# Cosine attention: queries and keys turned by 32x32 blocks and DMA instead of on TensorE, and output products held until after a projection's keys

## The chip, the cores and the metric

The kernel runs on one core of a Trainium2 chip (trn2). A core has TensorE (PE: matmuls; PEld: its weight loads), VectorE (DVE), ScalarE (ACT), GpSimd (POOL) and SyncE (SP, whose queue issues all the DMAs here). Each has its own list of instructions and works through it in order; waits between engines go by semaphores. The metric is the device time of one execution in microseconds (us). All data is float32.

## The reference

Four layers run one after the other on x of 8 batches x 256 rows x 512 features: a conditioned attention with MLP, a cosine attention with MLP, a sparse attention, and a layer of small experts. The change lies in the second layer's attention, 16 heads of 32 features:

```python
qkv = (xin @ Wqkv.T + qkv_bias).reshape(Bs, Lx, 3, H, D)
q, k, v = (qkv[0], qkv[1], qkv[2])
sm = jnp.exp(jnp.minimum(scale_mul_log, jnp.log(jnp.float32(100.0))))
qn = q / jnp.maximum(jnp.linalg.norm(q, axis=-1, keepdims=True), 1e-12) * sm
kn = k / jnp.maximum(jnp.linalg.norm(k, axis=-1, keepdims=True), 1e-12)
scores = jnp.einsum('bhqd,bhkd->bhqk', qn, kn) + attn_bias
p = jax.nn.softmax(scores, axis=-1)
o = jnp.einsum('bhqk,bhkd->bhqd', p, v)
return o @ Wproj.T + bproj
```

The layer adds this, times a factor gamma1 per batch and feature, to x.

## The kernel before

One Python program lays out the whole work. A tile framework allots buffers, sets the semaphores, and may reorder independent instructions on an engine by its own estimate of times; `keep_in_program_order` pins an instruction at its place on its engine. A buffer kind has a fixed number of copies (line 42): PSUM, where TensorE writes, has four banks "A" for scores and four banks "C" for everything else; hT, qT, kT and v have two copies each.

`attend` (line 655) runs an attention layer. Its main loop (line 838) goes over batch b and head group g: for the cosine layer 8 batches, and 4 groups of 4 heads. An iteration computes the scores of its group (`scored`, line 685: for each of two query tiles a product of 128 queries with 256 keys for each head, L697; the four heads fill the four A banks), then the softmax (line 706). There DVE adds the bias and takes the row minimum of the negated scores, reading an A bank (L743), and ACT exponentiates and sums (L747). To be weighted with the values the weights must be turned, keys to the partitions. For two of the four heads of a group (in all batches but the last) that goes over DRAM: DVE turns 32x32 blocks (L752), four DMAs write the tile to a DRAM buffer with the blocks rearranged (`put`, line 545, L549), and one fetches it back (L756); this is called a flip below. The other heads are turned on TensorE (L783). One group later the weighting follows (L808), and the division by the sums (L830).

Between these steps `some(us)` (line 208) takes work from a queue of generators, each of which yields its estimated time; `todo` us are planned per batch and spread over its steps. At the first group of a batch `rest` empties the queue. For the cosine layer the queue holds the projection of the next batch (`project1`, line 1458) and the output products of the last one (`finish`, line 1546), put at the queue's front when the last group has been weighted (line 909).

`project1` takes the input hT of its batch (normalised, turned by blocks over DRAM in `prepare` and `fetch`, and scaled in place in `modulate`, L490 and L491). For both tiles t of 128 rows it makes the products for queries and keys (L631), adds the query bias on DVE (L1495), squares on ACT (L1496, L1498), sums per head on DVE (L1501), raises to the power -0.5 on POOL (L1504), and scales on POOL (L1508). Then it makes the values (copied on ACT, L1516), and turns queries and keys on TensorE: `turned` (line 1476), four turns of 128x128 into one C bank (L1479), copied out alternately by DVE (L480) and ACT (L483) to qT and kT with features on the partitions. `finish` adds a bias to the output product on DVE (L1454) and gates and adds to x on POOL (L1455, L1456). The first batch is projected at the end of the first layer's MLP (`layer1_begin`, line 1582), with 22.1 us planned.

Of the kernel before, what the change touches and what calls it, by code (L numbers as in the profile page):

```python
# [27 lines left out]
F32 = mybir.dt.float32  # L28
# [60 lines left out]
ROUND = 1.5 * 2.0**23  # L89
PI_BELOW = 3.1415925  # L90


# [87 lines left out]
class Program:  # L180
# [50 lines left out]
    def setup(self):  # L231
# [39 lines left out]
        self.turns = [self.tc.dram_tile([P, KC * S], F32, name=f"turn{i}") for i in range(3)]  # L271
        self.n_turn = 0
        self.flips = [self.tc.dram_tile([P, 8 * P], F32, name=f"flip{i}") for i in range(4)]
        self.n_flip = 0
# [270 lines left out]
    def put(self, kept, tile):  # L545

        to = kept.rearrange("(c i) (a x) -> a i c x", c=4, a=4)
        for a in range(4):
            self.nc.sync.dma_start(  # L549
                to[a], tile[32 * a : 32 * a + 32, :].rearrange("p (c x) -> p c x", c=4)  # L550
            )

    def fetch(self, calls):

        for (name, b), entry in self.ready.items():
            hT, _, kept, _, _ = entry
# [98 lines left out]
    def attend(self, name, n_groups, hd, project, value, finish, work, key_tiles=(2, 2), biased=None,  # L655
               extra=None, then=None, spare=None, inverse=None, after=None, rooms=None, contexts=None):

# [27 lines left out]
        def scored(b, g):  # L685
# [3 lines left out]
            for j0 in range(0, 4, rows):  # L689
                for q in range(TB):  # L690
                    for j in range(j0, j0 + rows):
                        lhsT, rhs = lhs_rhs[j]
                        keys = rhs(wide[q])
                        if j < self.in_blocks(name, b):

                            keys = keys.rearrange("p (k c i) -> p c k i", c=4, i=32)
                        mm = nc.tensor.matmul(  # L697
# [122 lines left out]
        def divided(b, o, by):  # L820
            for c in range(nch):
                chunks = ctx.setdefault(b, [])
                if b == late:
                    out = spare()[len(chunks)]
                elif contexts is not None:
                    out = contexts[:, b % 2 * 4 + len(chunks), :]
                else:
                    out = self.t([P, S], "ctxT")
# [9 lines left out]
        for i in range(B * n_groups + 1):  # L838
# [59 lines left out]
            else:  # L898
# [368 lines left out]
    def project0(self, b, got):  # L1267
# [32 lines left out]
        def scores(g, j):  # L1300
# [3 lines left out]
                lambda q: qT[rows, c, q * P : (q + 1) * P],  # L1304
                lambda n: kT[rows, 0:n],
            )
# [49 lines left out]
    def layer0_mlp(self):  # L1356
# [54 lines left out]
        def finish(hh, b, ys):  # L1411
# [8 lines left out]
            lambda b: self.h("mlp0", b), finish,  # L1420
            (self.layer1_begin(), 22.1),
        )
# [35 lines left out]
    def project1(self, b, got):  # L1458
# [16 lines left out]

        def turned(t, y, yT, at):
            m = self.bank("C")
            for c in range(KC):
                nc.tensor.transpose(  # L1479
                    m[:, c * P : (c + 1) * P], y[:, c * P : (c + 1) * P], self.ident  # L1480
                )
# [4 lines left out]
        ready = []  # L1486
        for t in range(TB):
            ss = self.t([P, 32], "ss", 2)
            both = []
            for i in range(2):  # L1490
# [18 lines left out]
                both.append(y)  # L1509
            ready.append(both)  # L1510
        qT = self.t([P, KC, S], "qT")
        kT = self.t([P, KC, S], "kT")
        v = self.t([P, TB, D], "v")
        for t in range(TB):
            vp = yield from part(t, 2)
            nc.scalar.copy(v[:, t, :], vp)  # L1516
            if t == 0:
                turned(0, ready[0][0], qT, 0)
                yield 0.43
                turned(0, ready[0][1], kT, 1)  # L1520
                yield 0.43
        yield None
        turned(1, ready[1][0], qT, 0)
        yield 0.43
        turned(1, ready[1][1], kT, 1)
        yield 0.43

        def scores(g, j):
            rows = slice(32 * j, 32 * j + 32)
            return (  # L1530
                lambda q: qT[rows, g, q * P : (q + 1) * P],
                lambda n: kT[rows, g, 0:n],
            )
# [3 lines left out]
    def layer1_attention(self):  # L1537
# [128 lines left out]
    def project2(self, b, got):  # L1666
# [29 lines left out]
        def scores(g, j):  # L1696
            rows = slice(32 * j, 32 * j + 32)
            return (
                lambda q: qT[rows, g, q * P : (q + 1) * P],
                lambda n: kT[rows, 0:n],  # L1700
            )
# [4 lines left out]
    def layer2(self):  # L1706
# [10 lines left out]
            inverse=[spare[:, i, :] for i in range(4, 8)],  # L1717
            rooms=self.rooms, contexts=contexts,
        )
# [280 lines left out]
```

## Time and profile before

| | |
|---|---|
| median of three runs | 2081.69 us (2081.62 to 2082.62) |
| the profiled execution's own time | 2078.34 us |
| its span | 2076.6 us |
| cosine attention, groups of scores | from 907.2 us to some 1245 us |
| one batch in its middle | 43.66 us |
| TensorE's granted clock in the stage | 1.00 of full speed |
| busy in such a batch | PE 43.53, DVE 29.79, ACT 26.36, POOL 23.3 us |
| L1479, turns on TensorE | 128, records of 273 ns |
| L752, L534, block turns on DVE, 128x1024 | 1245 ns each |
| L1504, power on POOL, 128x16 | 32, 2931 ns each |
| L1508, scaling on POOL, 128x512 | 32, 1050 ns each |
| DMA in the stage | 54 to 55% of 16 engines, 141 GB/s |

A line Lnnn is a line of the kernel's text. An entry "PE C L631" is work of TensorE that writes to banks C, issued by line 631. A float32 product leaves two matmul records, a turn one. Records of matmuls overlap, so what one costs is read from the distance of their starts; and a busy PE may be waiting between records. In the chain of waits each piece is what the end of the work hung on at that time.

### The profile page before, as it was taken

How to read it: one execution, taken by the hardware profiler on the slowest of the kernel's cores; microseconds unless marked ns; L12 is line 12 of the kernel's file. 1: busy time of each engine (PE TensorE's matmuls, PEld its weight loads, DVE VectorE, ACT ScalarE, POOL GpSimd, SP SyncE). 2: the span in 40 equal slices, each digit the busy share in tenths (PEclk: the TensorE clock that was granted, in tenths of full speed). 3: DMA queues.
4: the chain of work that ended last, by engine and by line, in shares of the span. 5: the costliest groups of instructions: out<-in, count | busy, mean ns of one | idle time of the engine just before them, and what ended most of it. 6: DMA issues, size and time to landing. Idle time of an engine off the chain costs nothing.

```text
span 2076.6 us, 36333 instructions
## 1 busy us (share of the span) xinstructions
PE 2006.0 (97%) x12818; PEld 1480.9 (71%) x12818; DVE 1365.2 (66%) x4429; ACT 748.1 (36%) x2332; POOL 334.0 (16%) x372
## 2 busy tenths in 40 slices
PE   7999999999999999999999999999999989989999
PEld 4555579999999999954544447999999854445454
DVE  6867766656675555656676766776765678776544
ACT  4333421111111111136565653222222256565644
POOL 1111200000000000054544531000000021101411
PEclk9999999999999999999999999999999989999999
DMA  8543361112130010334555543233211245653411
GB/s 306 166 119 90 102 215 48 65 42 64 61 110 26 17 31 16 96 99 129 131 143 141 141 123 115 89 101 116 87 60 48 67 113 137 158 145 97 126 40 42
DMA packets 223685, 208.91 MB, mean 101 GB/s; under 512 B 83536, under 2 KB 184976, under 8 KB 223120
## 3 DMA queue, kind: packets, MB, share of 16 engines
q1 hardware_dynamic: 223504, 206.59, 34.3%
q8 instruction: 102, 1.67, 0.3%
q14 instruction: 79, 0.65, 0.1%
HBM read 135.46 MB, written 71.07 MB: 99 GB/s over the span
## 4 chain that ended last, share of the span: by engine, by line
PE 78%; DVE 7%; ACT 7%; DMA 4%; issue 2%; POOL 2%; SPq 1%; DVEq 0%; ACTq 0%; POOLq 0%
PE C L1024 29%; PE A L1073 18%; PE C L631 17%; PE A L697 3%; ACT p L747 3%; PE C L808 3%; ACT wbig L747 2%; PE C L783 2%; PE C L1887 2%; PE A L1789 1%; DMA turn<-hT 1%; PE C L1822 1%; DVE st L449 1%; DMA wbig<-in_wgT 1%; DVE n L650 1%
## 5 line engine op out<-in xcount | busy, mean ns | idle before, releaser
L1024 PE MATMUL C<-hT,wbig 128*128 128x128 f32 x3072 | 416.4, 275 | 0.0
L1024 PEld LDWEIGHTS C<-hT,wbig 128*128 128x128 f32 x3072 | 388.8, 192 | 9.0 <-issue 2.4
L631 PE MATMUL C<-wqkv,hT 128*128 128x512 f32 (+1 forms) x768 | 316.6, 553 | 0.9 <-ACT v L1516 0.4
L1073 PE MATMUL A<-wbig,p 128*128 128x256 f32 x1024 | 242.2, 379 | 0.0
L631 PEld LDWEIGHTS C<-wqkv,hT 128*128 128x128 f32 x768 | 134.0, 195 | 122.8 <-issue 108.5
L1073 PEld LDWEIGHTS A<-wbig,p 128*128 128x128 f32 x1024 | 189.7, 190 | 23.1
L1054 DVE TENSOR_TENSOR p<-p,C 128x256 f32<-128x256 f32 x192 | 79.3, 421 | 162.5 <-PE C L1024 160.8
L1044 ACT COPY p<-C 128x128 f32<-128x128 f32 x192 | 51.3, 267 | 370.3 <-PE C L1024 361.8
L1024 PE MATMUL C<-qk,wbig 128*128 128x128 f32 x1152 | 160.0, 275 | 0.0
L1024 PE MATMUL C<-ctxT,wbig 128*128 128x128 f32 x1152 | 160.0, 275 | 0.0
L457 POOL TENSOR_SCALAR r<-mv 128x2 f32<-128x2 f32 (+1 forms) x28 | 7.1, 254 | 929.0 <-DVE mv L450 929.0
L747 ACT ACTIVATE p<-p,low 128x256 f32<-128x256 f32 x256 | 127.3, 501 | 69.9 <-DVE low L743 48.4
L1024 PEld LDWEIGHTS C<-qk,wbig 128*128 128x128 f32 x1152 | 144.1, 192 | 0.0
L1024 PEld LDWEIGHTS C<-ctxT,wbig 128*128 128x128 f32 x1152 | 144.1, 192 | 0.0
L747 ACT ACTIVATE wbig<-wbig,low 128x128 f32<-128x128 f32 (+1 forms) x256 | 113.7, 448 | 78.9 <-DVE low L743 75.9
L1398 ACT ACTIVATE p<-C 128x128 f32<-128x128 f32 x64 | 17.8, 278 | 294.9 <-DVE p L1054 294.9
L1045 DVE TENSOR_TENSOR p<-p,C 128x128 f32<-128x128 f32 x192 | 55.0, 286 | 97.5 <-ACT p L1044 96.4
L631 PE MATMUL C<-wo,ctxT 128*128 128x512 f32 x224 | 103.1, 600 | 1.2 <-DVE ctxT L830 1.2
L1504 POOL TENSOR_TENSOR ss<-ss,neg_half 128x16 f32<-128x16 f32 x32 | 93.8, 2931 | 2.7
L747 ACT ACTIVATE p<-A,low 128x256 f32<-128x256 f32 x128 | 59.3, 486 | 87.0 <-DVE low L727 75.9
L697 PE MATMUL A<-kT,qT 32*128 32x256 f32 (+2 forms) x896 | 85.9, 399 | 1.4 <-ACT p L747 0.6
L697 PEld LDWEIGHTS A<-kT,qT 32*128 32x128 f32 (+1 forms) x896 | 52.4, 191 | 41.9 <-issue 29.0
(268 smaller groups left out, 3507.6 us busy)
## 6 DMA issues: line engine op xcount, KB each, us to landing
flip<-p SPq DMA_DIRECT2D x160, 128.0 KB
p<-flip SPq DMA_DIRECT2D x40, 512.0 KB
turn<-hT SPq DMA_DIRECT2D x120, 128.0 KB
flip<-wbig SPq DMA_DIRECT2D x112, 96.0 KB
wbig<-flip SPq DMA_DIRECT2D x28, 384.0 KB
hT<-turn SPq DMA_DIRECT2D x16, 512.0 KB
kept<-hT SPq DMA_DIRECT2D x16, 512.0 KB
hT<-kept SPq DMA_DIRECT2D x16, 512.0 KB
```

Source lines behind the costliest of these rows:

```text
L631: self.nc.tensor.matmul(out, lhsT(k), rhs(k), start=(k == 0), stop=(k == n - 1))
L697: mm = nc.tensor.matmul(s[j][:, at[q] : at[q] + wide[q]], lhsT(q), keys, start=True, stop=True,)
L747: nc.scalar.activation(out, src, AF.Exp, bias=low[:, q : q + 1], scale=sign, accum_out=tot[:, j, q : q + 1],)
L783: nc.tensor.transpose(m[:, n * P : (n + 1) * P], p[:, at[q] + k * P : at[q] + (k + 1) * P], self.ident,)
L808: mm = nc.tensor.matmul(o[i * hd : (i + 1) * hd, c * S + q0 * P : (c + 1) * S], value(got[b][1], g, j, k), weights(j, mine), start=(k == 0 ...
L1024: nc.tensor.matmul(m[:, c : c + P], w[:, k * P : (k + 1) * P], b[:, k], start=(first and k == 0), stop=(k == steps - 1), skip_group_check= ...
L1044: nc.scalar.copy(g[:, 0, :], m[:, 0:P])
L1045: nc.vector.tensor_tensor(g[:, 0, :], g[:, 0, :], m[:, P : 2 * P], ALU.add)
L1054: nc.vector.tensor_tensor(g[:, 1:3, :], g[:, 0, :].unsqueeze(1).to_broadcast([P, 2, P]), m[:, 2 * P : 4 * P].rearrange("p (i t) -> p i t", ...
L1073: nc.tensor.matmul(acc[at][:, half * S : (half + 1) * S], left, right, start=(p == 0 and half == 0), stop=(p == 3), skip_group_check=True,)
L1504: nc.gpsimd.tensor_tensor(r, r, self.neg_half[:, 0:16], ALU.pow)
L1887: nc.tensor.matmul(m[:, half * S : half * S + S], left[:, r, i, :], right[:, i, :], start=(first and i == 0), stop=(i == 1), skip_group_ch ...
```

## The change

Queries and keys of a projection are no longer turned on TensorE. POOL's scaling writes each row tile's queries and keys into one tile of 128x1024, ordered in 32-wide blocks: the tile of qT for the first 128 rows, that of kT for the others. DVE turns the 32x32 blocks of each such tile, and four DMAs write it to a DRAM buffer (`pairs`). The tile of the first rows is turned right after queries and keys; that of the second when 3.3 us (by the planner's count) of what follows have been given out. At 5.0 us four DMAs fetch: the queries of each row tile into a tile "qk", the keys of both into kT. At 9.0 us POOL copies the queries from there to qT. What is left at the projection's end is done then. The DVE turns and the POOL copies are pinned in program order. Keys stay in block order in kT, and the scores read them through a view in pieces of 32.

What follows queries and keys in a projection is now first the output products of the batch before, which `attend` holds back in `between` instead of putting them at the queue's front (for batches up to 5), and then the values. The contexts that wait for their output product lie in nine spare places in the second MLP's weight tiles, no longer in "ctxT". The projection is planned with 20.5 us instead of 22.1.

```diff
+def keys_of(keys, blocks):
+    return keys.rearrange("p (k c i) -> p c k i", c=4, i=32) if blocks else keys
...
+    def outputs_between(self):
+        while self.between:
+            yield from self.between.pop(0)
+
+    def turned_blocks(self, tile, kept):
+        self.tc.keep_in_program_order(self.nc.vector.transpose(tile, tile))
+        self.put(kept, tile)
...
-                        keys = rhs(wide[q])
-                        if j < self.in_blocks(name, b):
-                            keys = keys.rearrange("p (k c i) -> p c k i", c=4, i=32)
+                        keys = rhs(wide[q], j < self.in_blocks(name, b))
...
-                            self.queue.insert(0, outcome(b))
+                            if split and b + 2 < B:
+                                self.between.append(outcome(b))
+                            else:
+                                self.queue.insert(0, outcome(b))
...
-        def turned(t, y, yT, at):
-            m = self.bank("C")
-            for c in range(KC):
-                nc.tensor.transpose(
-                    m[:, c * P : (c + 1) * P], y[:, c * P : (c + 1) * P], self.ident
-                )
-            self.copy(
-                t + at, yT[:, :, t * P : (t + 1) * P], m.rearrange("p (c q) -> p c q", c=KC)
-            )
...
+        stages = [self.t([P, KC * S], tag) for tag in ("qT", "kT")]
+        keeps = [self.pairs[(self.n_pair + t) % 4] for t in range(TB)]
+        self.n_pair += TB
         for t in range(TB):
+            put = stages[t].rearrange("p (c w k i) -> p w k c i", c=4, w=2, k=KC)
...
-                by = r.unsqueeze(2).to_broadcast([P, 16, 32])
-                nc.gpsimd.tensor_tensor(heads(y), heads(y), by, ALU.mult)
+                by = r.rearrange("p (k c) -> p k c", c=4).unsqueeze(3)
+                nc.gpsimd.tensor_tensor(
+                    put[:, i], y.rearrange("p (k c i) -> p k c i", k=KC, c=4),
+                    by.to_broadcast([P, KC, 4, 32]), ALU.mult,
+                )
+        qT, kT = stages[0].rearrange("p (k t) -> p k t", k=KC), stages[1]
         v = self.t([P, TB, D], "v")
+        self.turned_blocks(stages[0], keeps[0])
+
+        def others():
+            yield from self.outputs_between()
+            for t in range(TB):
+                vp = yield from part(t, 2)
+                nc.scalar.copy(v[:, t, :], vp)
+
+        came = []
+        def fetched():
+            for t in range(TB):
+                kept = keeps[t].rearrange("p (a w x) -> p w a x", a=4, w=2)
+                came.append(self.bank("qk"))
+                nc.sync.dma_start(came[t].rearrange("p (a x) -> p a x", a=4), kept[:, 0])
+                nc.sync.dma_start(
+                    kT.rearrange("p (t a x) -> p t a x", t=TB, a=4)[:, t], kept[:, 1]
+                )
+        def placed():
+            for t in range(TB):
+                copy = nc.gpsimd.tensor_copy(
+                    qT[:, :, t * P : (t + 1) * P].rearrange("p k (a j) -> p k a j", a=4),
+                    came[t].rearrange("p (a k j) -> p k a j", a=4, k=KC),
+                )
+                self.tc.keep_in_program_order(copy)
+
+        way = [(3.3, lambda: self.turned_blocks(stages[1], keeps[1])), (5.0, fetched), (9.0, placed)]
+        done = 0.0
+        for us in others():
+            yield us
+            done += us or 0.0
+            while way and done >= way[0][0]:
+                way.pop(0)[1]()
+        for _, do in way:
+            do()
...
-            "attention1", 4, 32, self.project1, value, finish, (22.1, 6.8),
+            "attention1", 4, 32, self.project1, value, finish, (20.5, 6.8),
...
+            contexts=[self.downs[i][1][n] for i in range(1, 4) for n in range(3)], split=True,
```

More of the change, by code (lines that the diff above doesn't have):

```diff
@@ L272, in setup @@
         self.n_turn = 0
+        self.pairs = [self.tc.dram_tile([P, 8 * P], F32, name=f"pair{i}") for i in range(4)]
+        self.n_pair = 0
+        self.between = []
         self.flips = [self.tc.dram_tile([P, 8 * P], F32, name=f"flip{i}") for i in range(4)]
@@ L655, in attend @@
     def attend(self, name, n_groups, hd, project, value, finish, work, key_tiles=(2, 2), biased=None,
-               extra=None, then=None, spare=None, inverse=None, after=None, rooms=None, contexts=None):
+               extra=None, then=None, spare=None, inverse=None, after=None, rooms=None, contexts=None,
+               split=False):
         late = B - 3
@@ L825, in divided @@
                 elif contexts is not None:
-                    out = contexts[:, b % 2 * 4 + len(chunks), :]
+                    out = contexts[b % 2 * 4 + len(chunks)]
                 else:
@@ L1304, in scores @@
                 lambda q: qT[rows, c, q * P : (q + 1) * P],
-                lambda n: kT[rows, 0:n],
+                lambda n, blocks: keys_of(kT[rows, 0:n], blocks),
             )
@@ L1420, in layer0_mlp @@
             lambda b: self.h("mlp0", b), finish,
-            (self.layer1_begin(), 22.1),
+            (self.layer1_begin(), 20.5),
         )
@@ L1474, in part @@
             return m
-        def turned(t, y, yT, at):
-            m = self.bank("C")
-            for c in range(KC):
-                nc.tensor.transpose(
-                    m[:, c * P : (c + 1) * P], y[:, c * P : (c + 1) * P], self.ident
-                )
-            self.copy(
-                t + at, yT[:, :, t * P : (t + 1) * P], m.rearrange("p (c q) -> p c q", c=KC)
-            )
-        ready = []
+        stages = [self.t([P, KC * S], tag) for tag in ("qT", "kT")]
+        keeps = [self.pairs[(self.n_pair + t) % 4] for t in range(TB)]
+        self.n_pair += TB
         for t in range(TB):
+            put = stages[t].rearrange("p (c w k i) -> p w k c i", c=4, w=2, k=KC)
             ss = self.t([P, 32], "ss", 2)
-            both = []
             for i in range(2):
@@ L1506, in project1 @@
                     nc.gpsimd.tensor_tensor(r, r, self.sm, ALU.mult)
-                by = r.unsqueeze(2).to_broadcast([P, 16, 32])
-                nc.gpsimd.tensor_tensor(heads(y), heads(y), by, ALU.mult)
[L1509 to L1512, printed above, removed]
-        v = self.t([P, TB, D], "v")
[L1514 to L1526, printed above, removed]
+                by = r.rearrange("p (k c) -> p k c", c=4).unsqueeze(3)
[4 more added lines that the diff above has]
+        qT, kT = stages[0].rearrange("p (k t) -> p k t", k=KC), stages[1]
+        v = self.t([P, TB, D], "v")
@@ L1528, in scores @@
+        for _, do in way:
+            do()
+        kv = kT.rearrange("p (t a k j) -> p k t a j", t=TB, a=4, k=KC)
         def scores(g, j):
@@ L1531, in scores @@
                 lambda q: qT[rows, g, q * P : (q + 1) * P],
-                lambda n: kT[rows, g, 0:n],
+                lambda n, blocks: kv[rows, g].rearrange(
+                    "p t a j -> p a t j" if blocks else "p t a j -> p (t a) j"
+                ),
             )
@@ L1699, in scores @@
                 lambda q: qT[rows, g, q * P : (q + 1) * P],
-                lambda n: kT[rows, 0:n],
+                lambda n, blocks: keys_of(kT[rows, 0:n], blocks),
             )
@@ L1717, in layer2 @@
             inverse=[spare[:, i, :] for i in range(4, 8)],
-            rooms=self.rooms, contexts=contexts,
+            rooms=self.rooms, contexts=[contexts[:, i, :] for i in range(8)],
         )
```

## The prediction

> **What bounds the kernel now.** I read four views of the kernel before: the busy shares, the busy time in two stretches, the chain of waits over one batch of the cosine attention, and TensorE's (PE's) timeline at the start of that stage.
>
> Busy shares of the whole span, and busy time of each engine in two batches running (from the keys' products of one batch's first head group to those of the next):
>
> ```profile
> PE 2006.0 (97%) x12818; PEld 1480.9 (71%) x12818; DVE 1365.2 (66%) x4429; ACT 748.1 (36%) x2332; POOL 334.0 (16%) x372
> ```
>
> ```profile
> 1043.77:1087.43 43.66, 43.53 (x244) 21.29 (x244) 29.79 (x100) 26.36 (x85) 23.30 (x20) 1.00 0.55 141
> 1087.43:1131.09 43.66, 43.53 (x244) 21.29 (x244) 29.79 (x100) 26.36 (x85) 23.29 (x20) 1.00 0.54 141
> ```
>
> The columns are length, busy PE, PEld, DVE, ACT, POOL, PE's clock, DMA share and GB/s. PE is busy throughout; a batch takes 43.66 us, twice alike. So what the change takes from PE is gained, and what makes PE wait is lost, with nothing to hide it. The chain of waits across the seam between two batches:
>
> ```profile
> 1037.32 2.48 ACT p L747 x10
> 1039.80 0.47 ACT kT L483
> 1040.26 0.49 ACT p L483
> ...
> 1040.80 1.05 PE C L808 x10
> 1041.85 1.02 PE C L1479 x8
> 1042.87 0.90 PE C L783 x8
> 1043.77 1.07 PE A L697 x16
> 1044.84 7.06 PE C L631 x16
> ```
>
> L1479 is the turning that the change removes, and L697 the scores of a head group, which fill all four A banks of PSUM. Behind them lie 7.06 us of projection products: cover, while DVE empties the A banks for the next group. Where such cover is missing the timeline shows its price, at the first batch:
>
> ```profile
> 907.20 5.88 PE L697 MATMUL A<-kT,qT 32*128 32x256 f32 x26
> ```
> ```profile
> 908.96 0.42 DVE L743 CUSTOM_DVE_ANT_0 p<-A,wbig 128x256 f32<-128x256 f32 x1
> ...
> 909.30 0.42 DVE L743 CUSTOM_DVE_ANT_0 p<-A,wbig 128x256 f32<-128x256 f32 x1
> ...
> 911.37 0.42 DVE L743 CUSTOM_DVE_ANT_0 p<-A,row 128x256 f32<-128x256 f32 x1
> ```
>
> The 26 records are a group and most of the next, back to back (a product leaves two records). At 1.07 us per 16 they are 1.74 us of work, and they took 5.8: the second group waits for DVE to read the first one's banks, one read per 0.345 us. PE is shown as busy meanwhile.
>
> **What it removes.** 16 turns per batch, 128 in all. A record lasts 273 ns, but turns overlap: 8 take 0.88 to 0.93 us from start to start (the timeline around 1035 and 1042), so 0.113 us each, 1.8 per batch, 14.4 in all. The Trainium skill, "TensorE: Matmul & The Clock Gate", Part 4, gives some 275 ns for a 128x128 turn inside a kernel. Counted so, the gain would be 35 us, and with the losses below the kernel would come out unchanged; the starts decide, since PE is what is full: 14.4. Four evacuations go too (DVE 0.65 and 0.69, ACT 0.59 and 0.58 us per batch); one stands in the chain above with 0.47.
>
> **What it adds, per batch.** DVE: two block turns of 128x1024, each 1.245 us by the rows of L752 and L534, so +1.15 net; DVE is at 68%, no bound. POOL: two copies into the queries, 0.615 each by L1757's copy with a like pattern; the scaling now writes in blocks (1.05 as at L1508, at most 1.27 as at L1456): +1.2 to +2.1 beside 23.3 of 43.66. SP: eight writes of 128 KB and four fetches of 256 KB, at 0.44 and 0.34 us of issue some 4.9 us, and 2.1 MB, or 48 GB/s on 141. "VectorE: DVE Perf Modes", Rules for kernel authors, speaks against all this: a 128x128 turn belongs on TensorE where the result may go to PSUM. By the rows above the replacement takes 2.5 us of DVE where PE gave 1.8, but on an engine that has room; by engine time alone I would keep the change and forecast 2067. What decides is the order. Keys read in pieces of 32 (the new view) cost nothing: two of the four heads are read so now, and L697's records in the stage are 374 ns in the middle for all; bounds 0 and, should the pieces cost the 0.02 to 0.1 us by which single records differ, 0.1 per batch. I take 0.
>
> **What moves.** The changed program as built shows the order on each engine. In batches 1 to 7 PE's list now has the scores of groups 0 and 1 directly after each other, 16 products, where before a projection part lay between. The two parts that stood there (7 us) were put ahead of group 0, since queries and keys come late, over DRAM. From rows of before, with group 0's scores starting at T:
>
> Bank wait. DVE first reduces the squares of the part just ended (ACT 0.6, then 0.69), so the first score read starts near T+1.5. Bank j comes free 0.69(j+1) later; the last at T+4.4. Five products follow: PE is through at T+5.1 where the work is 2.15. Loss 2.9 a batch; the row at 907 (there DVE began 1.76 late) gives 3.5 for the whole. Bounds 2.4 (DVE free at T+1.1) and 3.3. Seven batches: +20.3.
>
> Input late. PE now wants the next input, hT, some 2.5 us sooner, before the scores. DVE scales half of it (L490), and its list has between the last group's block turn and that scaling: norms 1.0, a turn 1.25, statistics 1.5, a division 0.4. I get 10.3 us after group 3's scores start, and PE there at 8.8: up to 1.9; 0 if DVE is ahead. I take 1.4 for five batches: +7.
>
> Flips late. SP's list has the first write of group 1's flip (L549, waiting for DVE's turn) ahead of the fetch of group 0's flip. With both softmaxes run together that turn ends near T+11; the fetch needs some 4.2 us (issued 1217.81, awaited by PE until 1222.29), so T+15.6; PE wants it at T+15.0, in batch 1 already at T+10.5. 0.7 each and 5 there is 8.5; 0 if faster; I take 6.
>
> First batch. POOL ends its scaling at 903.5, and now follow DVE's turn 1.25, writes 1.8 and some 2 to land, then fetches behind the 1 MB of the output weights, and copies: scores at about 914 instead of 907.2. Against that the old start is itself slow (its turns of p begin at 917.4). Net of its own wait I take +2 (bounds -1, +5).
>
> Last batch. POOL's second query copy stands behind two gating steps (1.27 each) that wait for an output product just before the scores: +3 (0 to 6).
>
> Back. PE now waits about 1.2 us a batch before the weighting (L808 takes 1.48 and 1.74 for 1.0), partly on the evacuation that goes: -3 (0 to -8). The key fetch itself is no wait in the middle batches: it is issued some 6 us after group 3's scores start, the copies end near 12, and PE needs them at 15 or later. The added waits have work behind them: DVE's second turn waits for POOL's scaling, with group 3's score reads behind it (POOL ends near T+22.5, DVE comes near 22.8: 0, at most 1 per batch), and SP's fetches wait for the writes to land, with group 3's flip behind them (writes land some 5 us sooner: 0). Held output products cost nothing themselves; they are only moved between keys and values, and take the place of the turns as cover for DMA.
>
> Sum: -14.4+20.3+7+6+2+3-3 = +20.9. The profiled execution took 2078.34 us (span 2076.6), 3.4 under the median 2081.69, as such runs differ; I add the sum to the median: 2102.6.
>
> **Rivals.** (a) Faster: the turns' gain is whole and the seam costs little, 2081.7-14.4-3+2 = 2066. The point is a bank wait of 2.2 us per batch ((14.4+3-2)/7), with input and flips on time. For it: DVE and POOL have room. Against it: one read per 0.345 us sets at least 2.4. Chance 0.06; no change within 0.2% (about what a measurement can tell), 0.06.
> (b) Only the bank wait pays: -14.4+20.3-3+2 = +4.9, 2087, 0.2. For it: in this kernel DVE is often early.
> (c) The sum above, 2095 to 2112, 0.5.
> (d) Traffic: 190 GB/s and twelve more issues make flips and keys late in every batch, another 2 us each: 2117 and above, 0.18. For it: DMA share 0.55 already. Against: the span's first slice moves 306 GB/s.
>
> Low end: bank wait at 2.4, the rest near nothing, 2085. High end: the upper bounds together for most, 2117. Likeliest (c), 2102.6. Faster 0.06, same 0.06, slower 0.88.
>
> **What would show it.** In the profile after, no L1479; a batch of 46 to 47 us instead of 43.66; the scores of two groups as one stretch of 32 records taking 4.5 to 5.5 us; waits of PE for DVE's scaling of hT and for the fetch of the first flip; at the first batch scores near 914. I am wrong if those 32 records take under 3 us, or if the stretch is long and batches still are under 43.7.

## The result, and the profile after

The changed kernel took 2131.3 us in the median of four runs (2127.9 to 2136.9), the kernel before on the same chip 2081.65. The ratio is 1.0243, 95% interval 1.0219 to 1.0267: some 50 us slower, where the prediction said 21 and its range ended 35 above the kernel before. The profiled execution has a span of 2128.4 us, 51.8 over that of the kernel before.

The time is lost in the stage that was changed. The scores of batch 0 start at 917.3 us instead of 907.2, and the MLP behind the stage starts 55.7 us later than before; some 4 us of that are regained in it. The page's busy line:

```profile
PE 2015.0 (95%) x12690; PEld 1484.1 (70%) x12690; DVE 1377.9 (65%) x4429; ACT 740.5 (35%) x2316; POOL 341.4 (16%) x388
```

128 records fewer, and yet TensorE (PE) is busy 9 us longer and idle 43 us more. Which products pay is read from the groups of PE's instructions in the stage (905 to 1325 us). The columns are busy us, mean ns of a record, then idle us just before them and what ended that. First the kernel before, then the changed one:

```profile
L631 PE MATMUL C<-wqkv,hT 128*128 128x512 f32 x336 | 156.8, 604 | 0.4 <-ACT v L1516 0.4
L808 PE MATMUL C<-p,v 128*32 128x256 f32 x512 | 45.9, 387 | 5.0 <-ACT p L483 2.9 <-DMA p<-flip 0.9 <-DVE p L480 0.3
L697 PE MATMUL A<-kT,qT 32*128 32x256 f32 x512 | 45.7, 408 | 0.0
L783 PE MATMUL C<-ident,p 128*128 128x128 f32 x288 | 43.4, 281 | 0.9 <-DVE p L480 0.6 <-DVE n L1454 0.2
```
```profile
L648 PE MATMUL C<-wqkv,hT 128*128 128x512 f32 x336 | 162.2, 623 | 2.0 <-ACT p L491 2.0
L714 PE MATMUL A<-kT,qT 32*128 32x256 f32 x512 | 63.3, 459 | 25.4 <-DMA kT<-pair 14.1 <-DVE low L760 7.6 <-POOL qT L1551 3.6
L800 PE MATMUL C<-ident,p 128*128 128x128 f32 x288 | 46.7, 296 | 3.3 <-DVE wbig L847 1.9 <-DVE p L488 1.0 <-DVE n L1474 0.3
L825 PE MATMUL C<-p,v 128*32 128x256 f32 x512 | 46.4, 427 | 16.4 <-DMA p<-flip 13.4 <-DVE hT L478 1.4 <-ACT p L491 1.2
```

The lines have moved by some 17: L714 is the scores (L697 before), L825 the weighting (L808), L800 the turning of p (L783), L648 the projection (L631). Busy and idle together, the scores cost 43.0 us more, the weighting 11.9, the projection 7.0, the turning of p 5.7; the turns of queries and keys, 15.1 us busy in this stretch, are gone. That is +52.5 of the 55.7.

PE's timeline at the first batch and at the seam into batch 3 (start, us, and in brackets the idle time before, with what ended it):

```profile
917.27 2.09 PE L714 MATMUL A<-kT,qT 32*128 32x256 f32 x16 [10.59 <-DMA kT<-pair]
...
1074.01 1.15 PE L714 MATMUL A<-kT,qT 32*128 32x256 f32 x16
1076.32 3.10 PE L714 MATMUL A<-kT,qT 32*128 32x256 f32 x16 [1.17 <-DVE low L760]
1079.35 1.07 PE L825 MATMUL C<-p,v 128*32 128x256 f32 x16
```

The bank wait is there as forecast: 32 records from 1074.01 to 1079.35. PE stands 1.17 us, and the 16 records that follow take 3.10 us instead of 1.07, as the banks come free. Group 0's 16 records took 1.15 us, as before, so the keys in pieces of 32 cost nothing. What the flips met is in SyncE's (SP's) list, here around 1115 us in the changed kernel and around 1128 in the kernel before. A flip is written by four puts (flip<-p) and then fetched (p<-flip):

```profile
1111.08 0.55 SPq L1544 DMA_DIRECT2D qk<-pair  x1
1111.67 1.16 SPq L557 DMA_DIRECT2D flip<-p  x1
1114.56 0.54 SPq L1545 DMA_DIRECT2D kT<-pair  x1
...
1116.48 1.65 SPq L557 DMA_DIRECT2D flip<-p  x3
...
1121.37 0.34 SPq L773 DMA_DIRECT2D p<-flip  x1
```
```profile
1126.45 1.75 SPq L549 DMA_DIRECT2D flip<-p  x4
...
1130.33 0.78 SPq L756 DMA_DIRECT2D p<-flip  x1
```

After the first put SP stands at the fetch of the keys (L1545) until the pair's puts have landed, and three puts of the flip stand behind it. From the first put to the fetch this flip takes 9.7 us, in the kernel before 3.9. Over the stage the mean is 6.3 us against 4.3.

The flip shown, however, is that of group 3, the last of its batch, and PE does not wait for it. The changed kernel's weighting of groups 0, 2 and 3 of batch 3, and SP's list for the first two of these flips:

```profile
1090.32 1.07 PE L825 MATMUL C<-p,v 128*32 128x256 f32 x16 [0.87 <-DMA p<-flip]
...
1112.33 1.07 PE L825 MATMUL C<-p,v 128*32 128x256 f32 x16 [2.83 <-DMA p<-flip]
...
1127.73 1.93 PE L825 MATMUL C<-p,v 128*32 128x256 f32 x16
```
```profile
1079.43 1.75 SPq L557 DMA_DIRECT2D flip<-p  x4
...
1085.25 0.31 SPq L557 DMA_DIRECT2D flip<-p  x1
1085.78 0.34 SPq L773 DMA_DIRECT2D p<-flip  x1
...
1097.94 6.18 SPq L584 DMA_DIRECT2D hT<-turn  x8
1104.22 2.02 SPq L557 DMA_DIRECT2D flip<-p  x4
...
1108.56 0.34 SPq L773 DMA_DIRECT2D p<-flip  x1
```

PE waits for flips eight times, 13.4 us together. Five of these waits (batches 1, 3, 4, 5 and 6, 7.6 us) are for group 0's flip: its fetch, at 1085.78 here, stands behind the first put of group 1's flip, which waits for VectorE's turn. Two (batches 3 and 4, 4.7 us) are for group 2's flip: its puts stand behind the eight fetches of the next input (hT<-turn). VectorE had turned its weights by 1096.20, and the first put left at 1104.22; in the kernel before it left at once:

```profile
1094.95 1.25 DVE L769 STREAM_TRANSPOSE p<-p 128x1024 f32<-128x1024 f32 x1 [0.36 <-ACT p L764]
```
```profile
1071.92 1.25 DVE L752 STREAM_TRANSPOSE p<-p 128x1024 f32<-128x1024 f32 x1 [0.22 <-ACT p L747]
```
```profile
1073.20 1.76 SPq L549 DMA_DIRECT2D flip<-p  x4
```

The eighth wait, 1.1 us, is for the last flip of batch 6, whose puts and fetch took SP 3.8 us as before.

### The profile page after: what moved, and what is told of

The parts are those of the page before. It is cut to its first block, busy times and chain, and to the rows that moved or that the text cites. A ratio compares the mean times of both kernels' runs of the same rounds, so it can differ in the third digit from the quotient of the medians.

```text
span 2128.4 us, 36195 instructions
## 1 busy us (share of the span) xinstructions
PE 2015.0 (95%) x12690; PEld 1484.1 (70%) x12690; DVE 1377.9 (65%) x4429; ACT 740.5 (35%) x2316; POOL 341.4 (16%) x388
## 4 chain that ended last, share of the span: by engine, by line
PE 74%; DVE 8%; DMA 7%; ACT 5%; SPq 2%; POOL 2%; issue 2%; DVEq 0%; ACTq 0%; POOLq 0%
PE C L1044 28%; PE A L1093 18%; PE C L648 14%; PE A L714 4%; PE C L825 3%; ACT p L764 2%; PE C L800 2%; PE C L1931 2%; ACT wbig L764 2%; DMA turn<-hT 1%; PE A L1833 1%; DMA p<-flip 1%; SPq L584 1%; DVE st L457 1%; PE C L1866 1%
## 5 line engine op out<-in xcount | busy, mean ns | idle before, releaser
L648 PE MATMUL C<-wqkv,hT 128*128 128x512 f32 (+1 forms) x768 | 318.7, 557 | 3.7 <-ACT p L491 2.0
L648 PEld LDWEIGHTS C<-wqkv,hT 128*128 128x128 f32 x768 | 135.0, 196 | 128.2 <-issue 114.2
L648 PE MATMUL C<-wo,wbig 128*128 128x512 f32 x272 | 129.8, 607 | 0.0
L714 PE MATMUL A<-kT,qT 32*128 32x256 f32 (+2 forms) x896 | 102.5, 425 | 26.1 <-DMA kT<-pair 14.1
L1418 ACT ACTIVATE p<-C 128x128 f32<-128x128 f32 x64 | 17.7, 277 | 295.3 <-DVE p L1074 295.3
L714 PEld LDWEIGHTS A<-kT,qT 32*128 32x128 f32 (+1 forms) x896 | 63.7, 202 | 70.8 <-issue 36.6
```

The source lines that it names most:

```text
L648: self.nc.tensor.matmul(out, lhsT(k), rhs(k), start=(k == 0), stop=(k == n - 1))
L714: mm = nc.tensor.matmul(s[j][:, at[q] : at[q] + wide[q]], lhsT(q), keys, start=True, stop=True,)
```

## The experiments

Theory 1, formed on these traces: the loss is the order of PE's list at the batch seam, made by keys that come late, and the half clock that follows its gaps. Rivals: R1, the added load itself (VectorE, GpSimd, DMA, SP) slows the stage; R2, holding the output products is the cause. Later a theory 2 was added: the load acts through the order of SP's list, and not through the bytes. All ratios are to the kernel before, on the same chip.

| run | what it is | median us | ratio (95%) |
|---|---|---|---|
| after | the change | 2131.3 | 1.0243 (1.0219 to 1.0267) |
| e1_pinned | after, group order pinned | 2112.0 | 1.0169 (1.0149 to 1.0189) |
| e2_between_only | before, products held | 2078.2 | 1.0003 (0.9994 to 1.0012) |
| e3_first_pe | after, batch 0 on PE | 2130.0 | 1.0254 (1.0232 to 1.0275) |
| e4_no_between | after, nothing held | 2156.1 | 1.0378 (1.0354 to 1.0402) |
| e5_order_before | before, groups 0 and 1 back to back | 2104.6 | 1.0125 (1.0109 to 1.0140) |
| e6_load_before | before, load added on SP | 2104.4 | 1.0122 (1.0093 to 1.0150) |
| e7_pinned_poolq | e1, key fetches by GpSimd | 2124.2 | 1.0224 (1.0203 to 1.0246) |
| e8_pinned_ends | e1, batches 0 and 7 on PE | 2103.9 | 1.0126 (1.0103 to 1.0148) |
| e9_fill_order | e5, the gap filled | 2106.7 | 1.0134 (1.0119 to 1.0149) |
| e10_ends_late | e8, fetches later | 2133.3 | 1.0255 (1.0233 to 1.0277) |
| e11_ends_dve | e8, copies on VectorE | 2107.8 | 1.0138 (1.0122 to 1.0155) |
| e12_load_poolq | e6, load's DMAs by GpSimd | 2094.8 | 1.0075 (1.0048 to 1.0102) |
| e13_ends_actq | e8, key fetches by ScalarE | 2104.2 | 1.0115 (1.0092 to 1.0138) |
| e14_mid | batches 2 to 5 alone changed, 8 output products left out | 2088.0 | 1.0044 (1.0029 to 1.0058) |
| e15_mid_actq | e14, key fetches by ScalarE | 2091.6 | 1.0057 (1.0044 to 1.0070) |
| e16_mid_full | e14 with these products | 2090.9 | 1.0048 (1.0031 to 1.0065) |

**e1, order pinned on the changed kernel.**

```
-                        if name == "attention2" and j == q == 0:
+                        if name != "attention0" and j == q == 0:
                             self.tc.keep_in_program_order(mm)
```


> The changed kernel, with the first score product of each group of the cosine attention kept in its program's place on TensorE. In TensorE's list the groups 0 and 1 of batches 1 to 7 then stand apart (8 products, two projection chunks and a weighting, 8 products), where the change has 16 products back to back. Theory 1 (the loss is the order at the batch seam, and the half clock that follows its gaps): the wait for banks of about 3 us a batch goes (7 x 2.9 = 20 us), the 8 + 8 products no longer take T to T + 5.4 us, and the half clock that follows some of them goes too: 2095 to 2112 us. It could give less if the projection's parts now wait for hT right behind group 0. Rival R1 (the added DMA traffic and VectorE and GpSimd work slow everything): the order does little, 2122 to 2132 us. Rival R2 (holding the output products back is the cause): 2125 to 2132 us.

It took 2112.0 us, at the upper end of what theory 1 gave: about 15 us less than the change by the ratios (0.0074 of 2079, give or take 6 us by the intervals). In PE's list two projection products, the weighting and two more now stand between groups 0 and 1 in batches 2 to 5; in batches 1, 6 and 7 the 16 products stayed together. PE's waits for score reads fell from 7.6 to 3.0 us; those for flips stayed (14.0), and in two batches a wait of 2.2 us appeared ahead of hT's products (L648); the profile names no releaser, but it ends half a us into VectorE's scaling of hT (L498). One of the waits for flips, 2.6 us ahead of 1160.84, is now for a flip of group 3 that stood behind the key fetches. So the order costs, but it is not all.

**e2 and e4, holding the products.** e2 adds to the kernel before only the list `between`, the slots for the contexts and `yield from self.outputs_between()` ahead of the values; e4 takes `split=True` from the changed kernel.

> The kernel before with one part of the change alone: the output products are held and run between a projection's keys and its values; queries and keys are still turned on TensorE. Theory 1: no cost of its own, the scores keep their 8 and 8 places, 2079 to 2087 us. Rival R2 (holding the products is the cause): 2100 us or more.

> The changed kernel with the output products put back at the head of the queue (nothing held). Theory 1: there is then less work between queries, keys and the first scores, so the order at the seam stays bad or gets worse (two groups' 16 products still stand back to back in every batch): 2125 to 2145 us. Rival R2 (holding is the cause): 2085 to 2100 us. Rival R1 (load): as the changed kernel, 2128 to 2134 us.

R2 falls on both sides. Holding alone is no change within 0.12%; without it the changed kernel is some 28 us slower still by the ratios, more than theory 1 gave: PE waits there 37.7 us for keys and their copies, in the change 17.7. The likely reason is that less work is left to put between the keys' products and the scores.

**e3, batch 0 on TensorE.** `project1(0)` scales in place, turns queries and keys on PE as before, and returns.

> The changed kernel, with batch 0 alone turned on TensorE as before (its projection is not hidden behind anything). Theory 1: the first scores start near 907 instead of 917, without TensorE's 10.6 us of waiting for the first keys, and the half clock at their start stays as it was before: 2118 to 2123 us. Rival R1 (load): batch 0 adds an eighth of the load, so 2125 to 2130 us. Rival R2: no change, 2129 to 2133 us.

The first scores start at 906.0 and nothing is waited for there, but batch 1 starts at 962.2 instead of 968.0, 5.8 us earlier, not 10: the changed kernel had regained half by then. The median does not resolve it from the change and lies in R1's range, not in theory 1's: PE waits 17.8 us for flips here, against 13.4, which may be where the gain went.

**e5, the order alone, on the kernel before.**

```
-                ahead = (b, g, scored(b, g))
+                ahead = (b, g, early.pop(0) if early else scored(b, g))
...
                 ahead = (b, g, softmax(ahead[2], b))
+                if name == "attention1" and g == 0 and 0 < b:
+                    early.append(scored(b, 1, True))
```


> The kernel before, with nothing of the change but the order at the seam: in batches 1 to 7 the scores of group 1 are kept directly behind those of group 0 on TensorE. No added turns, no added transfers. Theory 1: the bank wait and what the reordering makes of it is there without any of the change's load, 2.9 to 3.5 us a batch, and the half clock behind some of them: 2097 to 2112 us, with 16 products that take T to T + 5.4 us in each batch. Rival R1 (load): 2079 to 2088 us.

2104.6 us, in the middle of theory 1's range: the order costs 26 us without one byte of the load. Its timeline at batch 4, its clock in three stretches of 25 us, and one of 2 us within the last (the last three columns are PE's granted clock, DMA share and GB/s):

```profile
1100.19 1.15 PE L697 MATMUL A<-kT,qT 32*128 32x256 f32 x16
1102.97 0.67 PE L697 MATMUL A<-kT,qT 32*128 32x256 f32 x2 [1.63 <-DVE low L743]
```
```profile
1050.00:1075.00 25.00, 23.25 (x125) 11.42 (x128) 16.73 (x56) 14.95 (x45) 7.87 (x8) 1.00 0.54 151
1075.00:1100.00 25.00, 24.88 (x152) 12.66 (x147) 16.54 (x51) 14.18 (x45) 15.45 (x13) 1.00 0.46 118
1100.00:1125.00 25.00, 23.37 (x107) 10.89 (x105) 13.89 (x51) 12.47 (x41) 7.95 (x8) 0.86 0.47 128
...
1107.00:1109.00 2.00, 2.00 (x4) 0.97 (x4) 0.03 (x1) 0.00 (x0) 0.00 (x0) 0.50 0.91 231
```

Group 0 starts at 1053.90, 1100.19, 1149.58 and 1195.86. The periods are 46.29, 49.39 and 46.28 us, against 43.66 before. So each of these batches pays 2.63 us of bank wait, and every second one 3.1 us more: there a stretch of 7 us, from group 1's last scores (about 1104.5) to 1111, ran at a clock of 0.50. Counted for the stage, seven waits and three such drops are 28 us.

**e9, the same order with the gap filled.** 14 turns of the identity, pinned behind group 0's scores, with a result that nothing uses.

> e5_order_before (the kernel before with the scores of group 1 directly behind those of group 0) with 14 idle transposes of the identity between the two groups on TensorE in batches 1 to 7; their result is not used. 14 at 0.113 us are 1.6 us, inside the bank wait of 1.6 to 2.2 us, so the wait itself is not longer. In e5's profile the time from one batch's first scores to the next alternates, 46.29 and 49.39 us, against 43.66 in the kernel before: 2.63 us of bank wait in every one and 3.1 us more in every second, where the granted clock of the stretch is 0.86. If the 3.1 us are TensorE's clock falling in the gap, they go: all periods at 46.2 to 47, no 0.86, 2096 to 2101 us, beside 2104.6. If they come from something else in that batch, they stay: 2103 to 2108 us.

```profile
1056.29 1.15 PE L697 MATMUL A<-kT,qT 32*128 32x256 f32 x16 [0.78 <-DVE kT L480]
1057.37 1.75 PE L860 MATMUL C<-ident 128*128 128x128 f32 x14
```
```profile
1050.00:1075.00 25.00, 24.10 (x133) 12.74 (x132) 17.34 (x56) 14.64 (x48) 5.39 (x6) 1.00 0.60 155
1100.00:1125.00 25.00, 24.10 (x133) 12.93 (x133) 16.70 (x55) 13.87 (x44) 6.66 (x7) 1.00 0.62 155
```

The clock stayed at 1.00 in six of seven batches and the alternation is gone: 1056.29, 1103.83, 1151.36, 1198.89, the three periods 47.5 us. So the drop belongs to the gap. The total did not fall, against what was expected. The period lies 3.88 us over the kernel before. 0.78 of it is a new wait for the keys' copy: four turns of p, its cover, had stood ahead of group 0 and moved behind it. The 3.1 left are the bank wait, with less of the kernel's own work inside it (those four turns, 0.45 us, where e5 has two records of a projection product, 0.86).

**e6 and e12, the load alone, on the kernel before.** Added beside the projection, on scratch tiles; e12 issues the added DMAs with `nc.gpsimd.dma_start`.

```
+        def out(t):
+            self.tc.keep_in_program_order(nc.vector.transpose(more[t], more[t]))
+            self.put(keeps[t], more[t])
...
+                    nc.sync.dma_start(more[t]..., keeps[t]...)
...
+                nc.gpsimd.tensor_copy(more[t][:, 384:768], more[t][:, 0:384])
```


> The kernel before with most of the change's load added beside it, for batches 1 to 7, on scratch tiles: two VectorE block turns of 128x768, eight puts to DRAM and four fetches back with as many packets as the change's (at three quarters of its bytes), on SP's queue, and two GpSimd copies of 128x384 for each batch; nothing waits for them, and the scores' 8 and 8 places stay. It computes the reference. Theory 1: load without the order costs little: 2080 to 2092 us, the upper end if flips queue on SP behind the added fetches. Rival R1 (the load is the cause): 2105 us or more.

> e6_load_before with the same added turns, puts, fetches and copies, but with the added puts and fetches issued by GpSimd and not by SP. The same bytes and packets move. TensorE's list is then again that of the kernel before. In e6 the time on SP from a flip's first put to its fetch is 8.65 us on average (4.3 in the kernel before). Theory 2 (the load costs through SP's list, in which a flip's fetch stands behind other transfers, and not through the traffic): that time is back at 4 to 5 us, TensorE's 14 us of waits for p<-flip go, 2080 to 2088 us. If the traffic itself slows the flips: 2095 to 2107 us.

e6 missed: 2104.4 us, where theory 1 gave at most 2092, and R1 at least 2105. In e6 the scheduler also moved group 0's weighting behind another group's scores, so it is not load alone. Its SP list, around 1065 us:

```profile
1053.08 4.65 SPq L1530 DMA_DIRECT2D wbig<-pair  x4
1058.19 1.95 SPq L551 DMA_DIRECT2D flip<-p  x4
...
1070.66 0.30 SPq L551 DMA_DIRECT2D flip<-p  x1
1071.18 0.34 SPq L758 DMA_DIRECT2D p<-flip  x1
```

The flip that was written at 1058.19 is fetched at 1071.18: its fetch stands behind the first put of the next flip, which waits for VectorE, as for group 0's flip in the change. With the same bytes issued by GpSimd, PE's waits for flips went:

```profile
PE C L810 <- DMA p<-flip: 13.9, 6, 4.2
```
```profile
PE C L810 <- DMA p<-flip: 1.1, 1, 1.1
```

(first e6, then e12: us in total, times, longest). From first put to fetch 8.65 us became 4.83. The time fell to 2094.8 us, not to the 2080 to 2088 of theory 2. So moving the issues gave about 10 of the 25 us back, with intervals that leave 2 to 18. It is not SP's list alone: in e12 TensorE's order is again that of the kernel before, and its clock in the stretches from 1025 to 1150 us is 1.00, in e6 0.93 to 0.99. The other 14 us are not settled, so R1, the load itself, stands for them. In three middle batches of e12 the period is 44.4 us, 0.7 over the kernel before, with a wait of 0.6 to 0.7 for the keys' copy; more lies in batches 1, 5 and 6. One caution: e6's fetches, in pieces of 384 bytes, took SP 1.16 us each, the change's, in pieces of 512, 0.54 to 0.63. So e6 overstates SP's part.

**e7, e10, e11, e13: four ways to relieve the queues.** e7 issues the key fetches by GpSimd, e13 by ScalarE (`nc.scalar.dma_start`), e10 moves the due points to `[(0.8, turn), (10.0, fetched), (12.5, placed)]`, e11 makes the copies with `nc.vector.tensor_copy`.

> The pinned kernel (e1_pinned) with the four fetches of queries and keys issued by GpSimd and not by SP. In e1_pinned SP issues the first put of a flip at 1051.73 and the other three at 1056.27, since the fetches of the keys stand between them and wait for the pair's puts. If the rest of the loss is SP's order (theory 2), TensorE's waits for p<-flip fall from 14 us to under 5, and it gives 2095 to 2105 us, beside about 2112 for e1_pinned. If it is not, it stays at 2108 to 2116 us; GpSimd held up by the same wait could delay its own work, up to 2120.

> e8_pinned_ends with the second turn's due point moved from 3.3 to 0.8 us and the fetches of queries and keys from 5.0 to 10.0, the copies from 9.0 to 12.5. On SP's queue the four puts of the last group's flip then stand ahead of the key fetches, where in e8 three of them stand behind a key fetch that waits until the pair's puts have landed. Theory 2 (the flips are late since SP's queue is held by that fetch): TensorE's waits for p<-flip fall from 16 us to under 8, and so do its waits for hT (4.4 us): 2088 to 2097 us. If the flips are late for the traffic itself, their wait stays, and the later keys cost something: 2102 to 2112 us.

> e8_pinned_ends with the two copies that place the queries on VectorE and not on GpSimd. In batch 1 TensorE waits 3.6 us in the middle of the first scores for GpSimd's second copy, which stands behind 2.93 us of power and 1 us of scaling; the 16 products of groups 0 and 1 stand apart there too then. Theory 1: batch 1 gets shorter by 5 to 9 us (3.6 of wait, about 3 of bank wait and the half clock behind): 2094 to 2099 us. If VectorE has no room at that place, 2101 to 2106 us.

> e8_pinned_ends with the four fetches of queries and keys issued by ScalarE and not by SP, so that SP's list has each flip's four puts together again and no key fetch ahead of them. Theory 2: the time from a flip's first put to its fetch falls from 5.85 to under 5 us, TensorE's waits for p<-flip from 16 to under 9 us, and the time to 2088 to 2098 us. If ScalarE's waits for the pair's puts hold up its exponentials instead, about the same as e8: 2100 to 2108 us. e7_pinned_poolq did this with GpSimd and lost more by late keys (32 us of waits) than the flips gave.

None gained: e13 is level with e8, and e7, e10 and e11 came out above every range given for them. e7 took the fetches off SP (first put to fetch 5.04 us), but on GpSimd they stood behind other work (in the batch at 1061 us behind a step of the next norm, which waited 6.7 us for VectorE): PE waited 31.8 us for keys instead of 13.5. e10 put the flips' puts together, and the keys came later: 10.7 us of waits for the copies, 20.4 for flips. e13 shortened the flips' way from 5.85 to 5.17 us, and PE still waited 15.8 us for them: 8.9 of these (batches 1 and 6) are for group 0's flip, whose fetch still stands behind the first put of the next flip. e11 took 3.6 us of wait for GpSimd away and made one of 9.7; VectorE's rows in batch 1:

```profile
959.22 0.43 DVE L1594 COPY qT<-qk 128x512 f32<-128x512 f32 x1 [2.71 <-DMA qk<-pair]
962.49 0.43 DVE L1594 COPY qT<-qk 128x512 f32<-128x512 f32 x1 [2.85 <-DMA qk<-pair]
962.84 0.73 DVE L498 TENSOR_SCALAR hT<-hT,mod 128x256 f32<-128x256 f32 x2
```

The copies wait for the fetches, and the scaling of hT, for which PE waits, stands behind them. A wait put on another engine takes along what is queued there.

**e8, e14, e15, e16: which batches.** `if b == 0:` of e3 becomes `if b in (0, B - 1):` in e8 and `if not 2 <= b <= B - 3:` in e14 to e16. e14 and e15 leave out the output products of batch 4; e16 has them. They are 16 records, 7.4 us of PE's busy time, about twice what the expectation of e16 took for them, so the times of e14 and e15 are lower than the whole layer's.

> The pinned kernel (e1_pinned) with the first and the last batch turned on TensorE as before (their projections have little beside them that could hide the way over DRAM). Theory 1: the waits for keys at both ends go (10.5 us and 3 us in e1_pinned's profile, of which e3_first_pe showed that the first gives back 5 to 6 us net), with the half clock behind them, and 3.6 us of turns come back: 2098 to 2106 us. If the ends are hidden anyway: 2110 to 2116 us.

> e8_pinned_ends with batches 1 and 6 also turned on TensorE: only batches 2 to 5 go by VectorE and DMA, group order pinned. In e8 the times between the first scores of batches 2 to 6 are 45.9, 46.0, 43.3 and 44.2 us against 43.66, and nearly all the rest of its 25 us lies around batches 1 and 6 (54 and 52.9 us). If that reading is right, the edges come back and it costs 2079 + 5 us for the four batches: 2081 to 2090 us. If the loss follows from any batch that is turned so, half of e8's loss stays: 2091 to 2098 us.

> e14_mid with the fetches of queries and keys issued by ScalarE. In e13 the same four periods are 44.5 us each, 0.9 us over the kernel before although 1.8 us of turns are gone: 2078 to 2086 us. Faster than the kernel before only if the wait for hT of 2.2 us at the seam, seen in e8 and e13, goes too (2074 to 2078 us).

> e14_mid with the output products of batch 4 put back: e14 and e15 left those 8 products of 0.43 us and their gating out, since the batches that are turned on TensorE did not run what was held. All of the reference is computed here. If e14's reading holds, it is e14's 2088 us and 3.4 us of products, with some of them filling e14's waits around batch 6: 2086 to 2093 us, against 2104 for e8, in which batches 1 and 6 also go by VectorE and DMA.

e8 gained 9 us on e1 by the ratios (give or take 6), as theory 1 said. e16 gained 16 more: with every batch but 2 to 5 on TensorE and the order pinned, 11.3 us over the kernel before remain, at the upper end of what was expected. Some 7 us of turns are saved there (64 at 0.113), so what four changed batches bring still loses 18. PE waits 14.2 us for flips in e16: 3.3 for group 2's, behind the fetches of the next input, 1.7 for a group 3's, behind the key fetches, 3.5 for group 0's, which took SP no longer than before (3.7 to 3.8 us), and 5.7 for two of batch 6. In e15 ScalarE as issuer gave nothing again; it came out above its range. No version beat the kernel before; the nearest is e16, at 1.0048.

## Why the prediction was wrong in size

The direction and the first mechanism were right; the sum was short by 29 us. By its steps:

**Turns, -14.4.** 15.1 us of busy time went from the stage. Right, and so was the choice of starts over durations.

**Bank wait, +20.3.** Right. In the changed kernel it is 7.6 us of idle time and, counted seven times, 3.10 - 1.07 us of paced scores, 21.8 together (three batches took 3.10 us; the other four, at a lower clock, 3.39 to 4.13). e5 shows it alone at 2.63 a batch.

**Failed: no term for the clock.** The sum priced each gap at its length. In e5 every second gap of 1.6 us is followed by 7 us at a clock of 0.50, which costs 3.1 us, more than the gap; e9 shows that filling the gap removes it in six of seven batches. In the changed kernel the projection, the turning of p and the weighting were busy 5.4 + 3.3 + 0.5 us longer for the same products. Of the scores' 17.6 the paced ones explain 14.2, so some 13 us in all. The profile before had shown it already at the first batch: its stretch of 25 us from 900 had a clock of 0.80. The Trainium skill, "TensorE: Matmul & The Clock Gate", Part 1, "A second HAM failure mode: psum-queue depth-cycling", describes the like for bf16 products: short idle times between groups of products that go round the PSUM banks make the clock swing. The same page, "Why this matters for your kernels", asks for no gap over some 3 us. By that rule this gap was safe; by the row, 1.63 us (and scores paced by the banks behind it) were enough every second time, and the row decides.

**Flips late, +6, and key fetches on SP, 0.** Both right as far as they went. The flip that the first term named, group 0's, with its fetch behind the first put of the next flip, costs 7.6 us in five batches (in batch 1 1.9 where the term had 5). The flip behind the key fetches, group 3's, took 9.7 us from first put to fetch, but PE does not wait for it in the changed kernel; with the order pinned (e1) it does once, 2.6 us.

**Failed: no term for group 2's flip.** Its puts stand behind the eight fetches of the next input, some 8 us in batch 3, which the prediction did not list. That is 4.7 us of PE's waits, or 6.2 if the 1.4 put down to VectorE (L478) ahead of the weighting of group 2 in batch 5 are for the same kind of flip.

**Failed in size: first batch, +2; last batch, +3.** The first keys were awaited for 10.6 us, net 5.8 at batch 1 (e3), though e3's median does not show that gain. Those of the last batch were awaited for 3.5 us, followed by half clock. From e1 to e8 both ends together are 9 us, and 3.6 us of turns came back with them: some 12.6 us of losses, of which about 3 are the bank wait of batch 7, so some 9.6 where the prediction had 5. With 6 us of uncertainty this is likely, not certain. GpSimd's copy behind power and scaling was foreseen for the last batch only; in batch 1 PE waits 3.6 us for it (L1551).

**Input late, +7.** Not there: PE's waits in the changed kernel do not name hT's scaling at all. With the order pinned the wait appears, 2.2 us in two batches of e1 and e8. That the slower front of the batch hid it is likely, not tested.

**Back, -3.** PE's wait for ACT ahead of the weighting fell from 2.9 to 1.2 us: -1.7.

The clock's 13 us, group 2's 5 to 6, GpSimd's 3.6 and some 5 at the ends, less the 7 of the input, are about 20 of the missing 29; the rest lies in smaller differences of every term. The range ended at 2117 because its upper bounds were those of the listed terms. A term that is not listed has no bound. Rival (d), 2117 and above, holds the result, and flips and keys were late as it said. Its cause, the traffic, is not shown: the middle batches moved 158 and 172 GB/s, not 190, and the waits traced above come from the order of SP's list. Nor is it excluded: e12's 14 us are not settled. For group 0's flips of e16, late without any delay on SP, the likeliest reading, not tested, is that PE has less work between a group's scores and its weighting, since the same projection products that covered flips now cover the keys.

## What to carry to other kernels

Where TensorE is the full engine, a turn that leaves it for DMA is paid with cover: the independent products that hide the new latency are taken from where they hid another, so look in the built order for what stands between producer and consumer afterwards. Price a TensorE gap at its length plus half the time that it may run at half clock afterwards (in e5 7 us of half clock cost 3.1). Before adding a DMA that waits for another one, list what is queued behind it on the issuing engine; moving the wait to another engine changed only who stood behind (e7, e11). Then ask of each transfer that is late whether an engine waits for it: the flip that was held longest here cost nothing, and others, held by transfers that nobody had looked at, did.

## What the runs showed of the hardware

An idle time of 1.63 us and scores paced by bank releases were enough to halve TensorE's clock for 7 us in batches 2, 4 and 6 of e5 and not in 1, 3, 5 and 7; the waits of batches 3 to 6 are the same within 0.01 us. Turns of the identity in the gap kept it at full speed in six of seven batches (e9). A DMA issued by GpSimd took 0.75 to 0.84 us of that engine (e7), by ScalarE 0.53 to 0.75 (e13), by SP mostly 0.54 to 0.63 for the same fetches. On SP's list a transfer that had to wait held up those behind it: a flip's fetch behind a put that waited for VectorE (13.0 us from first put to fetch in e6), a flip's first put behind eight fetches (8.0 us in the changed kernel).
